# Block transposes for five more heads' worth of probabilities, and a reordered tail, in a post-layer-norm attention and mixture-of-experts kernel

## The chip, the cores and the metric

The kernel runs on one core of a Trainium2 chip. The metric is device time in microseconds (us); three timed runs of the kernel before are listed below. Engines are named as in the profile: PE is TensorE (matmuls and transposes), DVE is VectorE, ACT is ScalarE, POOL is GpSimd, and SP is the engine that issues most DMAs.

## The reference, cut to what matters

All arrays are float32. The input x has shape (2, 1024, 256).

```python
# first layer, then a second layer-norm around the sum
x = layernorm(x + (attention_1_head(layernorm(x)) + x))      # causal, width 256
# second layer
a = attention(layernorm(x))          # 16 heads of 128, causal, rotary on q and k
h = x + a                            # a has the output projection wo and the bias bo
m = moe(layernorm(h))                # softmax gate, best 2 of 4 experts, 256 -> 256 -> 256, exact gelu
out = layernorm(x + (h + m))
```

For each head the second attention computes `scores = q k^T / sqrt(128)`, masks above the diagonal, takes a softmax over each row and multiplies the probabilities with v. Note that x enters the last line twice: once in h, and once as the residual around the layer.

## The kernel before, in words

**Units and steps.** Tokens are cut into 8 tiles of 128 rows per batch. The first layer has 16 rows of tiles (batch 0, then 1), the second has 32 units (a unit is one batch and one head) of 8 rows each. A row of tiles is a step: steps 0 to 15 are the first layer, and step A0 = 16 begins unit 0. Two units that share a batch and a group of weights make a pair; there are 16 pairs. `step(t, fillers)` writes out the instructions of a step in one fixed order, for all engines; each engine works through its own instructions in that order, so an instruction that waits holds up what is behind it on its engine. `at`, `mid`, `first`, `end_of`, `late` and `spread` hang other work onto steps: projections, weight loads, output projections, the first work of the mixture of experts.

**A row of attention.** `RowB.scores` (L703) multiplies q and k into a PSUM tile `sc` (two buffers). `softmax_row` takes the causal minimum (DVE, L329) and the row maximum (DVE, L331); ACT takes the exponential and its sum (L336). `normalise` takes the reciprocal (DVE, L715) and scales the row. Then the row's probabilities must be transposed, since the product with v (`output`, L773, tile `av`) contracts over the keys. There are two ways:

- The PE way (units 0 to 2 and 29 to 31): DVE scales the row (L719); `transposed_row` makes one PE transpose per 128x128 tile (L348), up to four into one PSUM tile, and ACT (L353) or DVE (L351) copies it to `pT`. The product with v follows three steps after the scores (lag 3).
- The block way (`self.blocks`, units 3 to 28, from `U0, U1 = 3, 29`): ACT scales the row (L717); DVE transposes 32x32 blocks (L728) into a staging buffer, `pair_sb` for rows 0 to 3 and the buffer of x1 for rows 4 to 7; and `gather` issues, on SP's queue, 16 DMAs for every four rows (L752) that bring the blocks to their places in `pT`. The product with v has lags of 8 to 10 steps (`PARTS`; lag 7 for unit 28).

Rows 0 to 3 and rows 4 to 7 of a unit are called its first and second half (j = 0 and 1). Row i has i + 1 tiles.

**Buffers with two uses.** The buffer x1 holds the first layer's result. `x1_out` stores it to DRAM (POOL's queue, step 42) before units 3 and later use the buffer for their blocks; `x1_back` loads it again in unit 29 (step A0 + 29*8 + 4). `pair_sb` also holds normalised tiles (`xn_tile`) before unit 3 and from unit 30 on.

**Around it.** `a_residual` finishes the first layer's normalisation in place in x1 (POOL, L438) and adds bo to make h (POOL, L441); for batch 1 this stands at steps 33 to 40. `seven_products` projects q, k and v with seven block products in place of eight; when `wide`, one of its accumulators is taken from the pool `ps_tr` and the order is another. `rotated` applies the rotary embedding to a finished half of q or k: two DMAs on SP's queue swap halves into `rot`, and one step later three POOL operations combine them (L479, L480, L481). `b_output` adds a pair's output projection to h.

**The tail.** From unit 30 on, batch 0's mixture of experts begins among the attention: `m_norm` normalises h (and has POOL add x1 to each tile of h, L1065), `m_transposed` and `gate_products` prepare it, and `hidden` (L1172, L1180) and `expert` (L1196, L1205) run experts 0 and 1 of the first half-batch at steps s + 2 to s + 6 of unit 31. What follows the last row is a list of calls written out by hand: `m_bias`, `m_stats`, `all_of` (one expert on four tiles: 16 matmul records and four DVE additions), and, last, batch 1.

Of the kernel before, what the change touches and what calls it, by code (L numbers as in the profile page):

```python
# [18 lines left out]
P = 128  # L19
# [7 lines left out]
def kernel(  # L27
# [377 lines left out]
    xn1, rr = {}, {}  # L405
# [15 lines left out]
    def a_rfinish(b, j):  # L421
        r = rr[b, j]
        nc.vector.reciprocal(r, r)
        xn1[b, j] = xn_tile()
# [9 lines left out]
    def a_residual(b, i):  # L434
# [3 lines left out]
        nc.gpsimd.tensor_scalar(  # L438
            t, t, mv_a[b][:, i, 0:1], rr[b, i // 4][:, 0, k : k + 1], ALU.subtract, ALU.mult
# [30 lines left out]
    def rotated(t, cs):  # L470
# [6 lines left out]
        def rest():  # L477

            nc.gpsimd.tensor_tensor(t[:, cs], t[:, cs], rope_sb[:, 0, cs], ALU.mult)  # L479
# [4 lines left out]

    BUFS = {"wq": 3, "wk": 4}
# [57 lines left out]
    def seven_products(g, b, name, wide):  # L543
# [46 lines left out]
        def done(i, k):  # L590
            if not value:
                rotated(head_tile(heads[i - 1], name), ts(k - 1, 512))
# [63 lines left out]
    def b_output(g, b, tiles):  # L656
# [17 lines left out]
    U0, U1, GP = 3, 29, 2  # L674
    R1, XB = 33, 4
    PARTS = (
        {8: range(0, 4)},
        {8: range(0, 2), 9: range(2, 4), 10: range(4, 8)},
    )
    LAGS = (11, 10, 9, 8, 7, 3)  # L680

    class RowB:


        def __init__(self, u, i):
            self.u, self.i = u, i
            k = units.index(u)
            self.blocks = U0 <= k < U1

            self.parts = {}  # L690
            if i % 4 == 3:
                self.parts = {3: range(i + 1)}
                if self.blocks:
                    self.parts = {7: range(i + 1)} if k == U1 - 1 else PARTS[i // 4]

# [190 lines left out]
    for i in range(NT):  # L886
        late(9 + i, a_residual, 0, i)
        late(R1 + i, a_residual, 1, i)
# [28 lines left out]
    for k, (g, b) in enumerate(pairs):  # L917
# [3 lines left out]
        wide = U0 <= k * GH < U1  # L921
# [19 lines left out]
        if k:  # L941
# [3 lines left out]
            else:  # L945
                spread(s0, own + outputs, (2, 2, 2, 2, 2, 2, 2, 1))
                at(s1, load_weights, g, ("wo",))
# [75 lines left out]
    def x1_out():  # L1023
        nc.gpsimd.dma_start(x1_dram, x1)

    def x1_back(b):
        nc.gpsimd.dma_start(x1[:, ts(b, NT), :], x1_dram[:, ts(b, NT), :])

    at(R1 + NT + 1, x1_out)
    for b in range(B):  # L1030
        at(A0 + U1 * NT + XB, x1_back, b)
    at(A0 + 28 * NT, load_second, range(3))
    at(A0 + 30 * NT + 4, load_second, (3,))
# [24 lines left out]
    def m_norm(b, j):  # L1058

        xn = xn_tile()  # L1060
        for k in range(4):
# [3 lines left out]
            nc.gpsimd.tensor_tensor(ht, ht, x1[:, b * NT + i, :], ALU.add)  # L1065
        xn2[b, j] = xn

# [183 lines left out]
    at(s + 4, hidden, 0, 0, 1)  # L1251
    at(s + 5, expert, 0, 0, [(0, k) for k in range(4)])
# [126 lines left out]
```

## Time and profile before

| | us |
|---|---|
| median of three runs | 1210.44 (1210.01, 1210.44, 1216.87) |
| the profiled execution's own time | 1212.35 |
| span of the profiled execution | 1210.6 |
| PE busy | 1173.9 |
| DVE busy | 786.9 |
| ACT busy | 633.7 |
| POOL busy | 614.7 |
| PE transposes of probabilities, both layers (L348, 288) | 43.9 |

The span runs from the first to the last instruction; 1.75 us of the profiled time lie outside it. Busy time of PE counts each matmul from its start to its modelled end, and consecutive matmuls overlap, so a long row of matmuls shows as one stretch. A float32 matmul is recorded as two instructions, a transpose as one. Where a unit begins is read from the first of its eight instructions on L329: unit 1 at about 159 us, unit 2 at 197, unit 3 at 231, unit 4 at 259, unit 5 at 284, unit 28 at 937, unit 29 at 969, unit 30 at 1007, unit 31 at 1047, and the last row of unit 31 at 1083.

### The profile page before, as it was taken

The page shows a single profiled execution, that of the slowest core. Times are in us where ns is not written, and L with a number is a line of the kernel's source. Part 1 is how long each engine was busy: PE and PEld are TensorE (multiplying, and loading weights), DVE is VectorE, ACT ScalarE, POOL GpSimd, SP SyncE. Part 2 cuts the span into 40 slices and gives each one's busy share as a digit, 9 for nine tenths or more (in the row PEclk, how much of TensorE's full clock was granted, in tenths as well). Part 3 has the DMA queues.
Part 4 walks back from the last instruction along what each step waited for, and adds up shares of the span by engine and source line. Part 5 has one row for each costly group of instructions (what it writes and reads, how often), then busy time and mean ns, then how long its engine had stood idle before and what let it go on. Part 6 is the DMA issues. An engine that isn't in the chain of part 4 may idle for free.

```text
span 1210.6 us, 15641 instructions
## 1 busy us (share of the span) xinstructions
PE 1173.9 (97%) x4570; PEld 744.1 (61%) x4570; DVE 786.9 (65%) x1810; ACT 633.7 (52%) x1181; POOL 614.7 (51%) x600
## 2 busy tenths in 40 slices
PE   7999989999999999999999999999999999999997
PEld 5676646565656566665656565656566557666665
DVE  5555657676666676666666666676676556677576
ACT  3344434566565565656565656665565544443423
POOL 4036379966564747384746556575848482101000
PEclk9999989999999999999999999999999999999999
DMA  5001112267766767667666676676767870000001
GB/s 180 1 1 36 31 31 61 53 200 161 167 159 156 164 152 166 146 158 161 157 155 162 160 161 157 165 168 159 171 154 173 171 201 32 34 1 1 18 17 35
DMA packets 210949, 140.18 MB, mean 116 GB/s; under 512 B 18764, under 2 KB 192912, under 8 KB 210480
## 3 DMA queue, kind: packets, MB, share of 16 engines
q1 hardware_dynamic: 207616, 129.05, 45.8%
q0 software_dynamic: 2160, 9.08, 2.1%
q10 hardware_dynamic: 1088, 1.05, 0.3%
q8 instruction: 37, 0.61, 0.2%
q14 instruction: 48, 0.39, 0.1%
HBM read 19.57 MB, written 4.19 MB: 20 GB/s over the span
## 4 chain that ended last, share of the span: by engine, by line
PE 88%; DVE 6%; DMA 2%; ACT 1%; SPq 1%; issue 1%; POOL 1%; DVEq 0%; POOLq 0%; ACTq 0%
PE av L773 21%; PE sc L703 19%; PE pa L563 11%; PE pa L660 7%; PE pa L554 5%; PE pc L563 4%; PE pa L1172 4%; PE pa L392 3%; PE sc L370 3%; PE pa L1196 2%; PE pt L348 2%; PE pc L554 2%; PE pe L1196 2%; DVE nmx L331 1%; PE pa L311 1%; PE pa L298 1%
## 5 line engine op out<-in xcount | busy, mean ns | idle before, releaser
L336 ACT ACTIVATE pr<-sc,nmx 128x128 f32<-128x128 f32 (+7 forms) x272 | 200.9, 739 | 190.9 <-DVE nmx L331 128.7
L703 PE MATMUL sc<-Twk,Twq 128*128 128x512 f32 (+3 forms) x768 | 290.6, 487 | 0.0
L773 PE MATMUL av<-pT,vg 128*128 128x512 f32 (+3 forms) x768 | 268.3, 489 | 6.9 <-DMA wq_g<-in_L_ffn_wq_dram 2.9
L717 ACT ACTIVATE pr<-pr,rs 128x128 f32<-128x128 f32 (+1 forms) x208 | 161.3, 775 | 149.9 <-DVE rs L715 149.8
L773 PEld LDWEIGHTS av<-pT,vg 128*128 128x128 f32 x768 | 143.1, 191 | 127.9 <-issue 98.8
L331 DVE TENSOR_REDUCE nmx<-sc 128x1 f32<-128x128 f32 (+7 forms) x272 | 206.1, 758 | 9.4
L703 PEld LDWEIGHTS sc<-Twk,Twq 128*128 128x128 f32 x768 | 138.9, 191 | 114.1 <-issue 101.2
L479 POOL TENSOR_TENSOR Twk<-Twk,rope_sb 128x512 f32<-128x512 f32 x64 | 81.6, 1275 | 222.6 <-DMA rot<-Twk 196.2
L329 DVE TENSOR_TENSOR sc<-sc,limit 128x128 f32<-128x128 f32 x272 | 79.9, 294 | 149.4 <-PE sc L703 136.0
L480 POOL TENSOR_TENSOR rot<-rot,rope_sb 128x512 f32<-128x512 f32 x128 | 165.1, 1290 | 0.0
L728 DVE STREAM_TRANSPOSE x<-pr 128x640 f32<-128x640 f32 (+1 forms) x104 | 108.0, 1039 | 39.1 <-DMA rot<-Twq 17.9
L660 PE MATMUL pa<-wo_g,aT 128*128 128x256 f32 x512 | 126.0, 380 | 0.6 <-ACT aT L789 0.3
L660 PEld LDWEIGHTS pa<-wo_g,aT 128*128 128x128 f32 x512 | 95.5, 190 | 33.7 <-issue 17.2
L479 POOL TENSOR_TENSOR Twq<-Twq,rope_sb 128x512 f32<-128x512 f32 x64 | 81.7, 1277 | 40.9 <-DMA rot<-Twq 30.4
L481 POOL TENSOR_TENSOR Twq<-Twq,rot 128x512 f32<-128x512 f32 x64 | 81.8, 1278 | 5.0
L481 POOL TENSOR_TENSOR Twk<-Twk,rot 128x512 f32<-128x512 f32 x64 | 81.2, 1269 | 5.0
L789 ACT ACTIVATE aT<-av,par 128x512 f32<-128x512 f32 x64 | 43.9, 686 | 64.4 <-PE av L773 64.4
L670 DVE TENSOR_TENSOR hx<-hx,pa 128x256 f32<-128x256 f32 (+1 forms) x124 | 52.2, 425 | 30.7 <-PE pa L660 28.9
L1065 POOL TENSOR_TENSOR hx<-hx,x 128x256 f32<-128x256 f32 x16 | 12.2, 791 | 103.6 <-DVE pair_sb L208 103.6
L588 ACT ACTIVATE part<-pa,par 128x512 f32<-128x512 f32 x64 | 43.8, 686 | 36.9 <-PE pa L563 36.8
L1172 PE MATMUL pa<-xT,we_sb 128*128 128x512 f32 x128 | 58.4, 596 | 2.0 <-DVE hx L1205 1.9
L728 DVE STREAM_TRANSPOSE pair_sb<-pr 128x128 f32<-128x128 f32 (+1 forms) x104 | 52.2, 502 | 3.5 <-DMA wq_g<-in_L_ffn_wq_dram 3.0
(194 smaller groups left out, 1690.4 us busy)
## 6 DMA issues: line engine op xcount, KB each, us to landing
pT<-x SPq DMA_DIRECT2D x416, 128.0 KB, 2.5
pT<-pair_sb SPq DMA_DIRECT2D x416, 64.0 KB, 2.0
rot<-Twk SPq DMA_DIRECT2D x128, 128.0 KB, 2.3
rot<-Twq SPq DMA_DIRECT2D x128, 128.0 KB, 2.3
wk_g<-in_L_ffn_wk_dram SPq DMA_DIRECT2D x9, 256.0 KB, 3.1
wq_g<-in_L_ffn_wq_dram SPq DMA_DIRECT2D x9, 256.0 KB, 3.5
wv_g<-in_L_ffn_wv_dram SPq DMA_DIRECT2D x9, 256.0 KB, 2.9
wo_g<-in_L_ffn_wo_dram SPq DMA_DIRECT2D x9, 256.0 KB, 2.9
```

Source lines behind the costliest of these rows:

```text
L331: nc.vector.tensor_reduce(nmx, sc[:, :L], AX.X, ALU.max, negate=True)
L336: nc.scalar.activation(pr[:, :L], sc[:, :L], AF.Exp, bias=nmx, accum_out=sm)
L479: nc.gpsimd.tensor_tensor(t[:, cs], t[:, cs], rope_sb[:, 0, cs], ALU.mult)
L480: nc.gpsimd.tensor_tensor(rot, rot, rope_sb[:, 1, cs], ALU.mult)
L481: nc.gpsimd.tensor_tensor(t[:, cs], t[:, cs], rot, ALU.add)
L563: nc.tensor.matmul(pa, lhsT=w, rhs=x, start=start, stop=True, skip_group_check=True)
L660: nc.tensor.matmul(pa[:, ts(k, D)], lhsT=aT[g, b][:, hh, ts(i, P)], rhs=wg["wo"][:, hh, :], start=(hh == 0), stop=(hh == GH - 1),)
L703: nc.tensor.matmul(sc[:, ds(n0, n)], lhsT=qT[:, ts(i, P)], rhs=kT[:, ds(n0, n)], start=True, stop=True,)
L717: nc.scalar.activation(self.pr[:, :L], self.pr[:, :L], AF.Copy, scale=rs)
L728: nc.vector.transpose(z[:, i % 4, :n, :], self.pr[:, : n * 32].rearrange("p (m s) -> p m s", s=32))
L773: nc.tensor.matmul(cut(av), lhsT=vg[g, b][:, c, ts(hh, HD)], rhs=cut(pT[:, c, :]), start=(c == 0), stop=(c == i),)
L1172: nc.tensor.matmul(ph, lhsT=we1_sb[:, e, c, ts(m, P)], rhs=x2T[:, c, ds(k0 * P, 512)], start=(c == 0), stop=(c == DC - 1),)
```

## The change

Unit 1, 2 and 29 take the block way for both halves, units 30 and 31 for their second half. That moves `x1_out` to steps 20 and 25, on ACT's queue, one batch each, and `x1_back` behind the last gather, on SP's queue. `a_residual` does its normalisation on ACT (with a small product `nb` on DVE for the bias), and batch 1's stands at steps 17 to 24. For the keys of pair 1 the first of the three rotary operations goes from POOL to DVE. Pair 1 becomes `wide`. In the last pair the value products are spread one to a row and the output projections move into unit 31; `hidden` of expert 0 moves into unit 30, that of expert 1 by one step, and the two experts' second products and four tiles of the output projection move behind the last row. The product with v for the second half of unit 31 is called by hand, behind expert 2's. POOL's addition of x1 moves out of `m_norm` into `m_residual`, called after `x1_back`.

```diff
 def a_rfinish(b, j):
         nc.vector.reciprocal(r, r)
+        nb = small.tile([P, 4], F32, tag=f"nb{b}{j}", name="nb", bufs=1)
+        nc.vector.scalar_tensor_tensor(
+            nb, mv_a[b][:, 4 * j : 4 * j + 4, 0], -1.0, r[:, 0, :], ALU.mult, ALU.mult
+        )
+        nbs[b, j] = nb
 def a_residual(b, i):
-        nc.gpsimd.tensor_scalar(
-            t, t, mv_a[b][:, i, 0:1], rr[b, i // 4][:, 0, k : k + 1], ALU.subtract, ALU.mult
+        nc.scalar.activation(
+            t, t, AF.Identity, bias=nbs[b, i // 4][:, k : k + 1], scale=rr[b, i // 4][:, 0, k : k + 1]
         )
         nc.gpsimd.tensor_tensor(h[:, b * NT + i, :], t, bo_sb, ALU.add)
-    def rotated(t, cs):
+    def rotated(t, cs, eng=nc.gpsimd):
-            nc.gpsimd.tensor_tensor(t[:, cs], t[:, cs], rope_sb[:, 0, cs], ALU.mult)
+            eng.tensor_tensor(t[:, cs], t[:, cs], rope_sb[:, 0, cs], ALU.mult)
+    HELP = ("wk",)
         def done(i, k):
-                rotated(head_tile(heads[i - 1], name), ts(k - 1, 512))
+                eng = nc.vector if (g, b) == pairs[1] and name in HELP else nc.gpsimd
+                rotated(head_tile(heads[i - 1], name), ts(k - 1, 512), eng)
-    U0, U1, GP = 3, 29, 2
-    R1, XB = 33, 4
-    PARTS = (
-        {8: range(0, 4)},
-        {8: range(0, 2), 9: range(2, 4), 10: range(4, 8)},
-    )
-    LAGS = (11, 10, 9, 8, 7, 3)
+    NU = B * H
+    U0, U1, GP = 1, (NU - 2, NU), 2
+    END = 99
+    PARTS = {
+        0: {8: range(0, 4)},
+        1: {8: range(0, 2), 9: range(2, 4), 10: range(4, 8)},
+        (NU - 3, 0): {7: range(0, 4)},
+        (NU - 3, 1): {9: range(0, 8)},
+        (NU - 2, 1): {7: range(0, 8)},
+        (NU - 1, 0): {4: range(0, 4)},
+        (NU - 1, 1): {END: range(0, 8)},
+    }
+    LAGS = (10, 9, 8, 7, 4, 3)
-            self.blocks = U0 <= k < U1
+            self.blocks = U0 <= k < U1[j]
...
-        late(R1 + i, a_residual, 1, i)
+        late(17 + i, a_residual, 1, i)
-        wide = U0 <= k * GH < U1
+        wide = 0 < k < len(pairs) - 1
-                spread(s0, own + outputs, (2, 2, 2, 2, 2, 2, 2, 1))
-                at(s1, load_weights, g, ("wo",))
+                spread(s0, own, (1, 1, 1, 2, 2, 0, 0, 0))
+                spread(s1, outputs, (0, 2, 2, 2, 2, 0, 0, 0))
+                at(s1 + 5, load_weights, g, ("wo",))
-    def x1_out():
-        nc.gpsimd.dma_start(x1_dram, x1)
+    def x1_out(b):
+        nc.scalar.dma_start(x1_dram[:, ts(b, NT), :], x1[:, ts(b, NT), :])
     def x1_back(b):
-        nc.gpsimd.dma_start(x1[:, ts(b, NT), :], x1_dram[:, ts(b, NT), :])
+        nc.sync.dma_start(x1[:, ts(b, NT), :], x1_dram[:, ts(b, NT), :])
-    at(R1 + NT + 1, x1_out)
-    for b in range(B):
-        at(A0 + U1 * NT + XB, x1_back, b)
+    at(A0 + 4, x1_out, 0)
+    at(A0 + 9, x1_out, 1)
-    at(A0 + 30 * NT + 4, load_second, (3,))
+    at(A0 + 30 * NT + 6, load_second, (3,))
 def m_norm(b, j):
-            nc.gpsimd.tensor_tensor(ht, ht, x1[:, b * NT + i, :], ALU.add)
+    def m_residual(b, tiles):
+        for k in tiles:
+            ht = h[:, b * NT + k, :]
+            nc.gpsimd.tensor_tensor(ht, ht, x1[:, b * NT + k, :], ALU.add)
+    mid(s - 2, hidden, 0, 0, 0)
-    at(s + 2, hidden, 0, 0, 0)
-    at(s + 4, hidden, 0, 0, 1)
-    at(s + 5, expert, 0, 0, [(0, k) for k in range(4)])
-    at(s + 6, expert, 0, 0, [(1, k) for k in range(4)])
-    at(s + 7, b_output, G - 1, 1, (0, 1))
-    at(s + 7, b_output, G - 1, 1, (2, 3))
+    at(s + 5, hidden, 0, 0, 1)
-    step(end, [lambda: hidden(0, 0, 2)])
+    step(end, [])
+    for i in (0, 2):
+        b_output(G - 1, 1, (i, i + 1))
     m_bias(0, (3, 4))
+    step(end + 1, [lambda: all_of(0, 0, 0)])
+    step(end + 2, [lambda: hidden(0, 0, 2)])
+    m_bias(0, (5,))
+    for b in range(B):
+        x1_back(b)
     m_stats(1, J0)
-    step(end + 1, [lambda: hidden(0, 0, 3)])
-    m_bias(0, (5,))
-    step(end + 2, [lambda: all_of(0, 0, 2)])
+    all_of(0, 0, 1)
+    hidden(0, 0, 3)
+    all_of(0, 0, 2)
+    steps[end - 1][0].output(END)
+    hidden(0, 1, 0)
     for i in (4, 6):
         b_output(G - 1, 1, (i, i + 1))
+    m_residual(0, ALL)
     m_stats(1, J1)
     m_sqrt(1, ALL)
-    hidden(0, 1, 0)
     m_rstd(1, ALL)
     m_norm(1, 0)
     m_norm(1, 1)
+    m_residual(1, ALL)
     all_of(0, 0, 3)
```

More of the change, by code (lines that the diff above doesn't have):

```diff
@@ L403, in output @@
                 a_finish(b, i // 4)
-    xn1, rr = {}, {}
+    xn1, rr, nbs = {}, {}, {}
     def a_finish(b, j):
@@ L686, in __init__ @@
             self.u, self.i = u, i
-            k = units.index(u)
-            self.blocks = U0 <= k < U1
+            k, j = units.index(u), i // 4
+            self.blocks = U0 <= k < U1[j]
             self.parts = {}
             if i % 4 == 3:
-                self.parts = {3: range(i + 1)}
-                if self.blocks:
-                    self.parts = {7: range(i + 1)} if k == U1 - 1 else PARTS[i // 4]
+                self.parts = PARTS.get((k, j)) or (PARTS[j] if self.blocks else {3: range(i + 1)})
         def scores(self):
```

## The prediction, made before the changed kernel was run

> **What bounds the kernel.** I read the page's busy shares, then busy time by stage (cut where units begin), then the waits of PE, then single instructions in order of time.
>
> ```profile
> PE 1173.9 (97%) x4570; PEld 744.1 (61%) x4570; DVE 786.9 (65%) x1810; ACT 633.7 (52%) x1181; POOL 614.7 (51%) x600
> ```
>
> PE is nearly always busy, but busy ends are modelled, so the stages decide. Columns: length, then busy time and count of PE, weight loads, DVE, ACT, POOL; granted clock; DMA.
>
> ```profile
> 159.00:197.00 38.00, 34.63 (x122) 19.45 (x120) 23.00 (x43) 15.77 (x34) 29.04 (x25) 0.91 0.24 56
> 197.00:231.00 34.00, 32.27 (x144) 20.17 (x144) 23.99 (x47) 15.29 (x33) 32.43 (x32) 1.00 0.17 40
> 231.00:259.00 28.00, 27.68 (x105) 17.34 (x105) 19.36 (x44) 15.27 (x32) 26.25 (x27) 1.00 0.56 178
> 259.00:284.00 25.00, 23.17 (x97) 13.97 (x96) 17.86 (x39) 16.32 (x31) 9.20 (x8) 1.00 0.65 148
> 284.00:314.00 30.00, 30.00 (x106) 18.58 (x105) 19.45 (x46) 17.32 (x33) 23.75 (x22) 1.00 0.73 167
> 314.00:341.00 27.00, 27.00 (x113) 16.79 (x112) 18.41 (x41) 17.58 (x34) 11.31 (x12) 1.00 0.70 157
> ...
> 1007.00:1047.00 40.00, 36.83 (x199) 27.25 (x197) 30.28 (x78) 17.77 (x36) 7.53 (x10) 1.00 0.08 27
> ```
>
> The rows at 284 and 314 are one settled pair of block units: PE has no idle time, DVE and ACT have 9 to 13 us to spare per unit. There a microsecond of PE work removed is a microsecond of time. The first rows are units 1 to 4, where the PE way ends and the block way begins: PE idles 7.25 of 125 us. The last row is unit 30, on the PE way.
>
> **The transposes that go.** A unit has 1+2+...+8 = 36 transposes, its second half 5+6+7+8 = 26; so 3x36 + 2x26 = 160 go.
>
> ```profile
> L348 PE MATMUL pt<-ident,pr 128*128 128x128 f32 x288 | 43.9, 279 | 3.6 <-DVE xT L217 1.5 <-DVE pT L351 1.0 <-ACT xT L219 0.8
> ```
> ```profile
> 1095.02 1.04 PE L348 MATMUL pt<-ident,pr 128*128 128x128 f32 x8
> ```
>
> The group gives 43.9/288 = 0.152 us each, which counts each burst's last latency. In order of time, eight take 1.04 and one alone 0.27, so each further one costs 0.77/7 = 0.11. PE runs on into other work, so I take 0.11: 160 x 0.11 = **-17.6** (bounds -17.6 and -24.4): 72 of them, -7.9, at the start, 88, -9.7, at the end.
>
> What takes their place: per full unit 16 block transposes in two shapes, whose means of 0.50 and 1.04 make 4x0.50 + 4x1.04 = 6.2 us on DVE, in place of 5.6 of scaling (L719, 0.70 x 8) and 1.9 of copies; ACT gains 8 x 0.775 = 6.2 and loses 8 x 0.50 of copies; SP gains 32 DMAs at about 0.65, 21 us in a unit of 28. The settled units carry exactly this with PE never idle, so I cost it at nothing there; it counts where PE has little other work, at both ends of the attention.
>
> The Trainium skill ("VectorE: DVE Perf Modes", Rules for kernel authors) speaks against the change: it gives a 128x128 transpose to TensorE when PSUM will do as the target, since DVE only turns 32x32 blocks, and its section on the three transpose paths warns of strided DMA copies. This trace has both ways: a row's block transpose takes 1.24 us against 1.04 for eight on PE, so by the rule the change gains nothing; but DVE has the room and PE has not, so I keep the row's answer.
>
> **Start (units 1 to 4).** Apart from the transposes only order changes: with lags of 8 to 10 the products with v leave unit 1 for later units, 2.6 us of them. The waits of PE there:
>
> ```profile
> PE pa L563 <- DVE Twk L595: 2.4, 1, 2.4
> PE pc L554 <- ACT part L586: 1.5, 1, 1.5
> PE pt L348 <- DVE xT L217: 1.5, 1, 1.5
> PE pa L563 <- DVE rs L715: 1.2, 1, 1.2
> PE pt L348 <- DVE pT L351: 1.0, 2, 0.7
> ```
>
> The 2.4 at 161 us is DVE's: two subtractions of x blocks (0.90, 1.75), unit 0's last scaling (1.56) and an addition. All stay, so it stays, and so does the slow clock behind it. The 1.0 waits on a copy of the PE way and goes; of the other 4.2 a light unit will have its like (unit 4, the first with little product work, has the 1.5 now). I take -2.5 in all for waits (bounds: +3, one more wait like the 2.4; -7, all idle time).
>
> POOL is busy 61.5 of 72 us in units 1 and 2. It loses 16 scalings in the first layer's residual (1.27 each), 8 of them at 207 to 245 us, and four rotary products (1.27 each, 5.1 us in unit 1); batch 1's eight additions (0.74, 5.9 us) come earlier, mostly into its gaps of 14 and 4.7 us. ACT's 16 residuals of 128x256 are bounded by its scaling of that size, 0.51, and its copy, 0.37: 6 to 8 us, in stages where ACT is busy 22 of 56 and 17 of 40 us; without that cover half a microsecond per step. The four products `nb` are 128x4, like L416 (0.67, twice 0.16): 1 to 3 us of DVE, hidden by PE. DVE's four rotary products have L540's shape: 0.68 to 1.75, so 3 to 7 us in unit 1. With them I count 26 us of DVE in unit 1 against 25 of PE, so unit 1 is even and its waits stay. `x1_out` took 8.8 us for both batches; the second, issued near 167, lands by 176, and the first block transpose into x1 is five steps later, near 181. Two issues on ACT's queue are 1 us. Start: -7.9 - 2.5 = **-10.4**.
>
> **End (unit 29 on).** Gains: -9.7, and waits of unit 30 that go because value products come one per row (1.1 on vg) and POOL no longer adds beside DVE's normalising (0.8; L208 takes 0.41 alone, 0.82 beside POOL): -2. `x1_back` leaves unit 29, where nothing waited for it.
>
> Losses: two places. **The last gather.** Counted from the end of the last scores on PE, DVE has: maximum 1.5, bias additions 4x0.52, block transposes of rows 5 and 6 (0.97, 1.11, with 1.0 of waiting for ACT's scaling), two output additions 1.3, bias additions 8x0.52, four expert additions 1.7, row 7's transpose 1.24: together 15. SP then issues 16 gathers at 0.65, 10.4, and the last lands 2.5 later:
>
> ```profile
> pT<-x SPq DMA_DIRECT2D x416, 128.0 KB, 2.5
> ```
>
> So the product may start at 28. PE has until then: first-half product 2.6 and six pieces of 3.45 (output projection, three expert products, two hidden layers): 23.3. PE waits about **+5** in all, in one piece or several (bounds: 0 if PE itself comes late, at 28; 10, the whole issue time). **The normalising chain.** Now, from the last output projection (PE ends at 1109.0) to the fourth normalised tile (1114.8) is 5.8 us, and two pieces on PE, 6.9, cover it. `hidden` of the next half moves ahead of the projection, so 3.45 cover 5.8: **+2.4**, and +0.6 for a PSUM bank freed later (0 to 4). `x1_back` (7.2 us) and POOL's first four additions (0.8 each) end near 28+10.4 = 39, before DVE's expert additions near 50; if they did not, DVE would wait, and PE with it. Sum of the end: -9.7 - 2 + 5 + 3 = **-3.7**.
>
> A wait of this size can cost more than itself:
>
> ```profile
> 161.60:164.10 2.50, 0.11 (x1) 0.00 (x0) 2.46 (x5) 0.00 (x0) 2.42 (x3) 0.79 0.00 0
> 164.10:167.00 2.90, 2.88 (x7) 1.74 (x8) 1.42 (x5) 1.69 (x4) 1.07 (x3) 0.50 0.41 90
> 167.00:170.00 3.00, 3.00 (x9) 1.88 (x8) 1.43 (x3) 0.62 (x2) 2.80 (x3) 0.52 0.00 0
> ```
>
> After 2.4 us without work the granted clock was half for 5.9 us: 2.9 us more. The waits of 1.7 and 1.5 had no such tail. I leave it out of the middle value and keep +3 in the range. The Trainium skill ("TensorE: Matmul & The Clock Gate", Part 1) puts the gate at an idle window of about 3.4 us; by it neither new wait would add anything, by the row one of them may add 2.9.
>
> **Sum.** -10.4 - 3.7 = -14.1. On the profiled execution's own 1212.35 that is 1198.2; this execution was 1.9 above the median of 1210.44, to which the same difference gives **1196**.
>
> **Rivals.** (a) *Nearly all of it comes through*: transposes at 0.11 to 0.152 and the start's waits gone, tail covered: -18 to -25, 1186 to 1192. For it: settled units hide all of this. Against: the tail has less cover. (b) *The tail eats its part*: gather 10 and chain 4, plus half clock 3, against -11.7: the end is +5, and the start alone remains: -5, 1205. (c) *Slower*: DVE's rotary products in unit 1 stand in order behind nothing but the `rot` transfers, in place of POOL, which idled 196.2 us in 34 waits for them, 5.8 each. If DVE waits 5.8 four times, PE (two score buffers) stops with it: 4x5.8, plus 2.9 of half clock each, is +35 against -14: 1231. It decides once a transfer lands later than DVE's arrival one step on by over 2 us. Against it: the transfer takes 2.3 and a step over 3; POOL merely came early. (d) *PE's time is not the limit at either end* (DVE and the queues are): the transposes leave as idle time, 0 to -4, 1208.
>
> **How the numbers follow.** Forecast (1190 to 1201) 0.54, (a) 0.15, (b) 0.18, (c) 0.07, (d) 0.06. The range leaves out (c), (d) and the outer part of (a): 1186 to 1207. About 1%, 12 us, is what a measurement of this kernel can tell: faster means under 1198.3. That takes two thirds to four fifths of the forecast and all of (a): 0.60; slower is (c), 0.07; the rest is 0.33.
>
> **What would show it.** L348 falls from 288 to 128 and unit 1's second half is in L728; units 1 to 4 take about 115 us together; the half clock of unit 1 is still there; PE waits ahead of the last product with v, with DMA named, and ahead of batch 1's transposes with L208 named. I am wrong if PE's waits in unit 1 name `rot`, if unit 29 is not near the 30 us of the settled unit at 284, or if the tail has more than 9 us of new waits.

## The result, and the profile after

| | us, median (lowest to highest) | runs |
|---|---|---|
| before, on the same chip | 1213.37 (1209.2 to 1218.47) | 12 |
| after | 1214.18 (1212.0 to 1217.75) | 12 |

The ratio is 1.0003, 95% interval 0.9985 to 1.0021: the change moves the time by nothing that can be measured, where 1196 was forecast. The profiled execution of after took 1212.0, with a span of 1210.2; of before 1212.35 and 1210.6.

The two profiles are not equally typical. The mean granted clock of after's 12 runs lies between 0.988 and 0.995 (median 0.991), and the profiled run, the fastest of them, has 0.995. Before's profile has 0.995 too, but the 30 runs of it that stand beside the first experiments have a median of 0.997. An estimate from these numbers: 0.006 of 1212, some 7 us of clock, is lost in a typical run of after and not in one of before, and the two profiles side by side do not show it.

The busy line of the page after:

```profile
PE 1158.6 (96%) x4410; PEld 727.3 (60%) x4410; DVE 782.1 (65%) x1798; ACT 652.0 (54%) x1197; POOL 587.1 (49%) x577
```

PE's busy time fell by 15.3 us and its instructions by 160, and the span stayed. The group of transposes (here with its releasers, from the groups of PE) has lost 160 of 288, as forecast, and gained a wait for the scaled row:

```profile
L348 PE MATMUL pt<-ident,pr 128*128 128x128 f32 x128 | 19.9, 276 | 7.3 <-DVE pr L732 5.4 <-DVE xT L217 1.5 <-ACT aT L802 0.3
```

The chain that ended last, by engine, before and after: a share of 14% of the span, 170 us, has gone over from PE to queues, transfers and the other engines. These shares say which way the chain runs, not what it costs: in the fastest kernel of the next section PE's share is 63%.

```profile
PE 88%; DVE 6%; DMA 2%; ACT 1%; SPq 1%; issue 1%; POOL 1%; DVEq 0%; POOLq 0%; ACTq 0%
```
```profile
PE 74%; SPq 8%; DVE 7%; DMA 5%; POOL 4%; issue 2%; ACT 1%; POOLq 0%; DVEq 0%; ACTq 0%
```

Busy time by stage after, cut where units 0, 1, 2, 3, 4, 5 and 6 begin and in the tail (columns as in the prediction):

```profile
119.00:165.00 46.00, 38.34 (x164) 25.42 (x162) 33.48 (x64) 22.04 (x43) 26.05 (x29) 1.00 0.16 46
165.00:195.00 30.00, 27.47 (x91) 14.32 (x92) 22.09 (x46) 16.04 (x32) 21.98 (x20) 1.00 0.36 99
195.00:226.00 31.00, 25.20 (x97) 14.87 (x97) 20.97 (x44) 17.10 (x33) 19.40 (x20) 0.94 0.66 153
226.00:261.00 35.00, 31.30 (x105) 18.73 (x104) 19.06 (x42) 17.05 (x33) 26.62 (x25) 0.95 0.81 175
261.00:288.00 27.00, 27.00 (x112) 16.63 (x111) 18.42 (x41) 17.29 (x34) 6.75 (x6) 1.00 0.57 131
288.00:318.00 30.00, 29.70 (x103) 18.11 (x102) 19.22 (x43) 16.85 (x32) 22.97 (x22) 1.00 0.72 166
...
1068.00:1210.00 142.00, 127.37 (x472) 85.63 (x470) 90.17 (x240) 45.91 (x60) 11.41 (x16) 0.98 0.15 45
```

PE now idles 7.7 us in unit 0 and 5.8 in unit 2, and in units 2 and 3 the granted clock fell to 0.94 and 0.95; unit 4 runs like a settled one. Busy ends are modelled, so for the comparison I count PE's own work in another way: each matmul at the median distance from its start to the next start for its shape, in that trace. What is left of a stage is waiting or slow clock. The count runs from PE's first to its last instruction, about 1199 us in both traces; what is left in the first and last cell of a column leaves out the time before and after. Each cell is length / what is left, in us, from one profile (start only, tail only and best kernel are kernels of the next section; the best one is its last).

| stage | before | after | start only | tail only | best kernel |
|---|---|---|---|---|---|
| up to unit 0 | 118.7 / 6.1 | 120.3 / 6.6 | 119.3 | 118.8 | 119.2 / 5.6 |
| unit 0 | 40.0 / 3.0 | 45.1 / 9.1 | 45.1 / 9.2 | 40.0 | 39.8 / 3.8 |
| unit 1 | 38.5 / 7.2 | 29.7 / 3.1 | 29.9 | 38.7 | 30.8 / 4.8 |
| unit 2 | 34.0 / 2.4 | 31.1 / 8.4 | 32.3 / 9.7 | 34.1 | 28.7 / 5.3 |
| unit 3 | 27.8 / 0.4 | 35.1 / 5.6 | 34.8 / 5.6 | 28.8 | 31.0 / 1.6 |
| unit 4 | 25.4 / 2.4 | 26.7 / 0.0 | 27.0 | 24.9 | 26.8 / 0.0 |
| units 5 to 27 | 652.9 / 6.0 | 652.5 / 4.8 | 653.8 | 654.5 | 655.8 / 8.9 |
| unit 28 | 31.5 / 4.8 | 28.0 / 1.0 | 28.6 / 1.8 | 32.8 / 6.1 | 27.9 / 1.3 |
| unit 29 | 38.2 / 0.8 | 30.9 / 1.6 | 40.5 | 29.5 | 30.6 / 1.1 |
| unit 30 | 39.7 / 4.7 | 36.5 / 5.8 | 39.6 | 37.4 / 6.8 | 35.3 / 4.7 |
| unit 31 | 36.4 / 1.6 | 32.3 / 1.7 | 36.4 | 32.3 | 32.3 / 1.7 |
| after the last scores | 127.5 / 4.5 | 142.2 / 12.8 | 127.3 | 141.9 / 12.3 | 136.6 / 7.2 |

In all, PE's own work fell from 1155.1 to 1138.7, by 16.4, and the rest rose from 43.9 to 60.3, by 16.4. The gain is there and is given back whole, mainly at four places: unit 0 (+6.1), unit 2 (+6.0), unit 3 (+5.2) and the tail (+8.3); units 1, 4 and 28 lost 10.3 us of waiting on the other side. The longest waits of PE in units 0 to 5 after:

```profile
PE pt L348 <- DVE pr L732: 5.4, 3, 2.5
PE av L786 <- DMA pT<-pair_sb: 4.1, 1, 4.1
PE av L786 <- DMA pT<-x: 3.7, 1, 3.7
PE pc L561 <- ACT part L593: 1.7, 1, 1.7
```

and from unit 29's end on:

```profile
PE pa L1190 <- DVE hx L1223: 4.8, 3, 2.0
PE av L786 <- DMA pT<-pair_sb: 3.3, 1, 3.3
PE av L786 <- DMA pT<-x: 2.9, 2, 1.6
PE pt L214 <- DVE pair_sb L208: 1.3, 3, 0.5
```

At three of the four places the name at the head is new: the scaled row and, twice, a gather. PE waited for the experts' sums in before's tail too, but less:

```profile
PE pa L1172 <- DVE hx L1205: 1.9, 2, 1.5
```

Behind some of the waits the granted clock was half for 3.4 us, a loss of 1.7 us each time. After has three such stretches, behind the waits of 4.1, 3.7 and, in the tail, 2.0; behind the wait of 2.5 in unit 0, which ends at 165.3, there is none:

```profile
165.30:168.70 3.40, 2.23 (x11) 1.35 (x11) 3.33 (x8) 2.12 (x5) 3.24 (x6) 1.00 0.09 39
208.00:211.40 3.40, 3.40 (x7) 1.86 (x6) 2.19 (x6) 1.29 (x3) 3.32 (x4) 0.50 0.94 224
255.80:259.20 3.40, 3.40 (x6) 1.44 (x5) 2.38 (x5) 2.14 (x3) 3.32 (x5) 0.50 0.59 135
1119.30:1122.70 3.40, 3.40 (x11) 2.05 (x9) 0.00 (x0) 1.28 (x2) 0.00 (x0) 0.51 0.00 0
```

Before has 6.8 us of half clock from 163.0 and 3.4 from 951.5, of which PE was waiting for 1.1. So the two profiles happen to lose nearly the same by it: about 4.6 us before, 5.1 after. The experiments ask who makes each wait long.

### The profile page after: what moved, and what is told of

The parts are those of the page before. It is cut to its first block, busy times and chain, and to the rows that moved or that the text cites. A ratio compares the mean times of both kernels' runs of the same rounds, so it can differ in the third digit from the quotient of the medians.

```text
span 1210.2 us, 15511 instructions
## 1 busy us (share of the span) xinstructions
PE 1158.6 (96%) x4410; PEld 727.3 (60%) x4410; DVE 782.1 (65%) x1798; ACT 652.0 (54%) x1197; POOL 587.1 (49%) x577
## 4 chain that ended last, share of the span: by engine, by line
PE 74%; SPq 8%; DVE 7%; DMA 5%; POOL 4%; issue 2%; ACT 1%; POOLq 0%; DVEq 0%; ACTq 0%
PE av L786 18%; PE sc L716 14%; PE pa L570 8%; SPq L765 7%; PE pa L668 6%; PE pa L561 5%; PE pa L1190 4%; PE pc L570 3%; DMA pT<-x 3%; PE sc L370 3%; PE pa L392 2%; PE pc L561 2%; PE pe L1214 1%; PE pa L1214 1%; DVE pair_sb L208 1%
## 5 line engine op out<-in xcount | busy, mean ns | idle before, releaser
L786 PE MATMUL av<-pT,vg 128*128 128x512 f32 (+3 forms) x768 | 272.1, 493 | 18.7 <-DMA pT<-x 8.8
L730 ACT ACTIVATE pr<-pr,rs 128x640 f32<-128x640 f32 (+1 forms) x240 | 187.7, 782 | 179.4 <-DVE rs L728 179.2
L485 POOL TENSOR_TENSOR Twk<-Twk,rope_sb 128x512 f32<-128x512 f32 x60 | 76.4, 1273 | 199.2 <-DMA rot<-Twk 175.7
L741 DVE STREAM_TRANSPOSE x<-pr 128x640 f32<-128x640 f32 (+1 forms) x124 | 128.8, 1039 | 54.4 <-DMA pT<-x 32.0
L485 POOL TENSOR_TENSOR Twq<-Twq,rope_sb 128x512 f32<-128x512 f32 x64 | 81.5, 1273 | 46.0 <-DMA rot<-Twq 27.3
L802 ACT ACTIVATE aT<-av,par 128x512 f32<-128x512 f32 x64 | 43.9, 686 | 46.1 <-PE av L786 46.1
L595 ACT ACTIVATE part<-pa,par 128x512 f32<-128x512 f32 x62 | 42.6, 687 | 39.5 <-PE pa L570 39.4
L741 DVE STREAM_TRANSPOSE pair_sb<-pr 128x128 f32<-128x128 f32 (+1 forms) x116 | 58.2, 502 | 3.6 <-issue 3.4
L447 POOL TENSOR_TENSOR hx<-x,bo_sb 128x256 f32<-128x256 f32 x16 | 12.2, 763 | 99.5 <-ACT x L444 99.5
```

The lines of the kernel that those rows point to most:

```text
L485: eng.tensor_tensor(t[:, cs], t[:, cs], rope_sb[:, 0, cs], ALU.mult)
L730: nc.scalar.activation(self.pr[:, :L], self.pr[:, :L], AF.Copy, scale=rs)
L741: nc.vector.transpose(z[:, i % 4, :n, :], self.pr[:, : n * 32].rearrange("p (m s) -> p m s", s=32))
L786: nc.tensor.matmul(cut(av), lhsT=vg[g, b][:, c, ts(hh, HD)], rhs=cut(pT[:, c, :]), start=(c == 0), stop=(c == i),)
```

## The experiments

**The two halves apart.** First the start alone, made from before: block way from unit 1, residual on ScalarE and 16 steps earlier, rotary products for pair 1's keys on VectorE, `x1_out` early (the diff shows only the steps). Then the tail alone, made from after with all of that undone.

```diff
-    U0, U1, GP = 3, 29, 2
-    R1, XB = 33, 4
+    U0, U1, GP = 1, 29, 2
+    R1, XB = 17, 4
```
```diff
-    U0, U1, GP = 1, (NU - 2, NU), 2
+    U0, U1, GP = 3, (NU - 2, NU), 2
-    HELP = ("wk",)
+    HELP = ()
-        late(17 + i, a_residual, 1, i)
+        late(33 + i, a_residual, 1, i)
```

> The kernel before with the start of the change alone: blocks from unit 1 on, the first layer's residual on ScalarE and at steps 17 to 24, the two early stores of x1, DVE's part of the key rotation, pair 1 wide; the tail as before. Theory S (the start's removed transposes, 72 x 0.11 = 7.9 us, come back as new waits in units 0, 2 and 3): units 0 to 4 take 167 to 169 us as in the changed kernel (before 165.8), the whole within 4 us of before. Rival R (the start gives the 10 us of the prediction, and it is lost by what the start does to the tail): 8 to 11 us faster than before.

Measured: 1219.24 (1215.33 to 1223.54, 8 runs) against 1211.6 (30 runs) of before, ratio 1.006 (1.0039 to 1.0082). The start alone costs 0.6%, so rival R falls. Theory S has units 0 to 4 right (169.1 us), but not the whole: 7.6 us slower, where S allowed 4. Its profile shows 3.4 of them in units 0 to 4 and 2.3 in unit 29; the profiled run is 2.6 us faster than the median, and the rest was not looked for. Its column shows the waits of units 0, 2 and 3 in full, and unit 28's wait gone: so that gain comes with the start and not with the tail.

> The changed kernel with the start of before (blocks from unit 3 on, residual on GpSimd at steps 33 to 40, one store of x1 at step 42) and the changed tail. Theory S: units 29 to the end as in the changed kernel, 242 us against 241.7 before, so the whole within 3 us of before; the 3.5 us that unit 28 gained in the changed profile, if they come with the tail, make it up to 4 us faster. Rival R: 10 us slower than before.

Measured: 1210.87 (12 runs), ratio 0.9993 (0.9979 to 1.0008). The tail alone is worth nothing either: units 29 to 31 are 15 us shorter (99.2 for 114.3) and what follows them 14.4 longer, of which 7.8 is waiting. The two halves fail independently. Their costs do not add up, though: +7.6 and -0.7 stand against about +1 for both together, and why is open.

**Unit 2: the gather of unit 1's first half.** PE comes to the product with v at 203.5; the last transfer lands at 207.3. The issues on SyncE's queue after, in order of time (the second column is the time that all of a row's issues took):

```profile
190.74 6.26 SPq L765 DMA_DIRECT2D pT<-pair_sb  x8
197.12 0.53 SPq L480 DMA_DIRECT2D rot<-Twq  x1
197.69 0.59 SPq L481 DMA_DIRECT2D rot<-Twq  x1
198.40 0.52 SPq L467 DMA_DIRECT2D wk_g<-in_L_ffn_wk_dram  x1
199.06 0.46 SPq L480 DMA_DIRECT2D rot<-Twq  x1
199.56 0.60 SPq L481 DMA_DIRECT2D rot<-Twq  x1
200.20 5.59 SPq L765 DMA_DIRECT2D pT<-pair_sb  x8
```

The gather's second eight stand behind the query's transfers and a weight load. So they were issued at once, right behind the first eight:

```diff
+                if row.u == units[1] and row.i == 3:
+                    if k == 0:
+                        row.gather(0)
+                        row.gather(1)
```

> The changed kernel, with both halves of the gather of unit 1's first four rows issued in one step, ahead of the two key or query swaps and the weight load that stand between them now. Theory Q (SP's queue in order: the second eight gathers stood behind transfers that waited for products of the next step): the wait of 4.1 us at unit 2's first product with v falls under 1.5, the half clock behind it goes, units 0 to 4 lose 4 to 6 us. Rival P (PE is early there, with little product work in units 1 and 2, and the gather begins only after DVE's fourth transpose): the wait stays above 3 us, nothing gained.

Measured: 1219.19 (9 runs), ratio 1.0051 (1.0035 to 1.0068). The wait for the gather fell to 0.3, as theory Q has it, but units 0 to 4 took 171.4 us (167.7 in after): a longer wait stands in its place.

```profile
PE sc L716 <- POOL Twq L487: 6.7, 2, 6.0
```

Now the query's transfers stand behind 16 gathers, the rotation comes late, and the scores wait 6.0 us. The queue takes one issue after another, and unit 2, with 22.7 us of its own work, reaches both needs before the queue has served either. My reading is that whichever goes second loses.

**Unit 3: the experts' load.** Unit 3's wait is for `pT<-x`, unit 2's second half, whose first eight gathers are issued from 236.5 on. At 235.3 GpSimd issues `load_experts`, 1 MB, which the change left at step A0 + 24, where no gather was before. It was moved to step A0 + 5:

```diff
-    at(A0 + 3 * NT, load_experts)
+    at(A0 + 5, load_experts)
```

> The changed kernel with the load of the experts' first weights (1 MB) 19 steps earlier, at step A0+5, where no gather runs. Theory C (in unit 3 that load slows the gathers: they land 8 us after their issue instead of 2.5): the wait of 3.7 us in unit 3 goes with its half clock, 4 to 6 us less. Rival I (the 16 issues at 0.65 us and the swaps on SP's queue are too slow for the lag by themselves): the wait stays above 2.5 us, at most 1 us less.

Measured: 1210.28 (10 runs), ratio 0.9982 (0.9961 to 1.0003), which does not tell it from before. Unit 3 falls from 35.1 to 29.5 with nothing left over. The transfers of that stretch, from issue to landing, after:

```profile
pT<-x SPq DMA_DIRECT2D x9, 128.0 KB, 7.2
we_sb<-in_L_ffn_we_dram POOLq DMA_DIRECT2D x1, 1024.0 KB, 9.3
```

and with the load moved away:

```profile
pT<-x SPq DMA_DIRECT2D x8, 128.0 KB, 2.6
```

The load on another queue made a gather take 7.2 us instead of 2.6, and SyncE's next issues late as well (the second eight begin at 246.45, without the load at 243.93): shown, since this load is the only thing that was moved. The second eight, all issued after the load had landed at 244.5, still took 4.4 us (2.4 without it).

**Unit 0: GpSimd's order.** GpSimd's addition of bo (L447) follows ScalarE's new residual (L444) in batch 1, and stands ahead of its rotary products. After, GpSimd and VectorE:

```profile
139.53 0.73 POOL L447 TENSOR_TENSOR hx<-x,bo_sb 128x256 f32<-128x256 f32 x1 [12.02 <-ACT x L444]
140.22 1.26 POOL L485 TENSOR_TENSOR Twk<-Twk,rope_sb 128x512 f32<-128x512 f32 x1
141.44 1.27 POOL L486 TENSOR_TENSOR rot<-rot,rope_sb 128x512 f32<-128x512 f32 x1
142.79 1.26 POOL L487 TENSOR_TENSOR Twk<-Twk,rot 128x512 f32<-128x512 f32 x1
```
```profile
140.49 1.02 DVE L426 SCALAR_TENSOR_TENSOR nb<-mva,rx 128x4 f32<-128x4 f32 x1
141.43 2.78 DVE L208 TENSOR_SCALAR pair_sb<-x,mva,rx 128x256 f32<-128x256 f32 x2
```

Before, GpSimd's three rotary products ran from 136.65 to 140.5 and VectorE's two normalising pieces after them, at 140.96, took 0.73 together. After, they run side by side and the pieces take 2.78 (1.44 and 1.42), each ending 0.15 us behind a GpSimd instruction of 1.27; the row's scaling stands behind them. So the additions were put two steps later:

```diff
-        nc.gpsimd.tensor_tensor(h[:, b * NT + i, :], t, bo_sb, ALU.add)
+        if b == 0:
+            a_bias(b, i)
+        late(19 + i, a_bias, 1, i)
```

> The changed kernel, with GpSimd's 8 additions h = x1 + bo of batch 1 put two steps later than ScalarE's residual, so that GpSimd's queue does not stand waiting for ScalarE (in the changed kernel it waits until 139.53 us and its rotary products then run at 140 to 150 us, beside VectorE's normalising pieces, L208, of 1.36 to 1.44 us each; before they were 0.41). Theory T1 (GpSimd's queue, held by ScalarE, slides onto VectorE): the pieces come back near 0.41 us, the waits of unit 0 for the normalised row (5.4 us in 3) mostly go, unit 0 falls from 45.1 to 40 or 41 us; the wait of unit 1 for the rotated k may come back (up to 2.4). Rival (the added work on ScalarE and VectorE itself is what costs): unit 0 stays at 45 us, within 1.

Measured: one run of 1207.24 beside one of 1208.64 of before; the stage decides. Unit 0 is 39.5 us (45.1), GpSimd's first product starts at 136.16, and VectorE's pieces:

```profile
140.47 0.23 DVE L426 SCALAR_TENSOR_TENSOR nb<-mva,rx 128x4 f32<-128x4 f32 x1
140.63 0.73 DVE L208 TENSOR_SCALAR pair_sb<-x,mva,rx 128x256 f32<-128x256 f32 x2
```

T1 holds: ScalarE's and VectorE's added work is all still there and costs nothing that unit 0 shows (40.0 in before); the wait that it put into GpSimd's queue cost 5.6 us.

**Unit 2 again: the product a step later.** With the experts' load early as well:

```diff
+        (1, 0): {9: range(0, 4)},
```

> The changed kernel with the experts' load early (as in the run before) and the attention product of unit 1's first half one step later, nine steps after its row instead of eight. Theory Q (SyncE's queue holds the gather, landed 207.3 us, when the light unit 2 wants it at 202.9): one step of unit 2 is about 3.2 us, so the wait falls from 4.1 us to about 1, the half clock after it goes, unit 2 falls from 31.1 to about 27 or 28 us and nothing else moves; units 0 to 4 about 158 us. Rival (the wait only moves on to the next product or to the scores behind the query's transfers, as with the gather in one step): unit 2 stays within 1.5 us of 31.

Measured: 1210.52, one run, before 1208.64. Unit 2 stays at 31.0: the rival is right. The product no longer waits; the scores do, for the rotated query:

```profile
PE sc L717 <- POOL Twq L487: 3.9, 2, 3.2
```

That the transfers for it landed at 202.7 and the rotation began at 204.6 shows who is next: GpSimd's four instructions on the sums of wk (L537 to L540), which had themselves waited for their weights until 202.2, stand ahead of it.

**The tail: the last row first.** After, VectorE ahead of the last block transpose:

```profile
1074.66 1.26 DVE L678 TENSOR_TENSOR hx<-hx,pa 128x512 f32<-128x512 f32 x2
1075.85 4.00 DVE L1177 SCALAR_TENSOR_TENSOR hx<-lent,comb,hx 128x256 f32<-128x256 f32 x8
1079.76 0.87 DVE L1223 SCALAR_TENSOR_TENSOR hx<-pe,comb,hx 128x256 f32<-128x256 f32 x2
1080.54 0.87 DVE L1223 SCALAR_TENSOR_TENSOR hx<-pa,comb,hx 128x256 f32<-128x256 f32 x2
1081.33 1.24 DVE L741 STREAM_TRANSPOSE x<-pr 128x1024 f32<-128x1024 f32 x1
```

The row was scaled by 1076.0 and stood 5.3 us behind the bias and an expert's sums.

```diff
-    m_bias(0, (3, 4))
-    step(end + 1, [lambda: all_of(0, 0, 0)])
+    step(end + 1, [])
+    all_of(0, 0, 0)
     step(end + 2, [lambda: hidden(0, 0, 2)])
-    m_bias(0, (5,))
+    m_bias(0, (3, 4, 5))
```

> The changed kernel with the last row's block transpose on VectorE ahead of two pieces of the experts' bias (8 instructions of 0.48 us) and of the first expert's combination. Theory L (the last row is late because VectorE's order puts 3.8 us of bias and the combination ahead of it): the transpose ends about 77 us instead of 82.6 (counted from 1000), the gather lands about 90 instead of 95.2, the product's wait of 1.6 us and the 1.5 us wait for hx before it go, and the tail is 2 to 3 us shorter (142.2 to about 139.5). Rival (TensorE finds other waits on VectorE there, which has the same work to do before it): tail within 1 us of 142.2.

Measured: 1214.68, one run, before 1208.64; the tail 141.5 (142.2). The transpose ran 5.3 us earlier and both waits went, as L has it; but the bias now stands ahead of the second expert's sums, and PE waits 2.05 for those (5.4 in 3 for hx, where after had 4.8). The rival is right: a wait on VectorE's order was moved, not removed.

**The tail: GpSimd's residual additions.** `m_residual` runs beside the last normalising, as the additions in `m_norm` did in before. The eight pieces took as long there (first line: before; second: after), but PE then waited only 0.4 us on them:

```profile
1112.64 5.14 DVE L208 TENSOR_SCALAR pair_sb<-hx,mvh,rsh 128x256 f32<-128x256 f32 x8
1111.61 5.13 DVE L208 TENSOR_SCALAR pair_sb<-hx,mvh,rsh 128x256 f32<-128x256 f32 x8
```

```diff
-    m_residual(0, ALL)
     m_stats(1, J1)
...
     m_norm(1, 1)
-    m_residual(1, ALL)
     all_of(0, 0, 3)
+    m_residual(0, ALL)
+    m_residual(1, ALL)
```

> The changed kernel with GpSimd's 16 residual additions (0.72 to 0.82 us each) put after the last normalising and the fourth expert's combination, so that none runs beside VectorE's normalising pieces. Theory S (a VectorE piece of 0.41 us takes 0.81 when GpSimd's two-input addition runs beside it): the six slow pieces come back to 0.41, the last ends 2.4 us earlier, the waits for them (0.40 and 0.40) go and the 2.0 us wait for hx shrinks by about 1.5: tail shorter by 1.5 to 2.5 us, unless the sums are then late for the output. Rival (VectorE is slow there for another reason): pieces stay at 0.81, tail within 0.5 us.

Measured: 1210.98, one run, before 1208.64; the tail 138.7 (142.2), more than S expected. The eight pieces:

```profile
1114.19 2.68 DVE L208 TENSOR_SCALAR pair_sb<-hx,mvh,rsh 128x256 f32<-128x256 f32 x8
```

S holds: 5.13 to 2.68 us, and the waits behind them go from 3.3 to 0.9. The half clock behind the wait of 2.0 goes with it, 1.7 us, which S did not count. So this run shows a cure, not what the change made worse: the slow pieces were there before, with more work of PE over them.

**All together.** The cures that held, and for the places where the wait only moved, the next one behind it: the sums of wk three steps later, the first expert's products ahead of the output projection, all of the bias in VectorE's idle time behind the last gather. For unit 30's 3.3 us, the first eight of unit 29's gather went to another queue.

```diff
-                at(before + (1 if k == 1 else 4), weight_sums, "wk")
+                at(before + 4, weight_sums, "wk")
+                    q = nc.scalar if (units.index(self.u), j, part) == (NU - 3, 0, 0) else nc.sync
+    all_of(0, 0, 0)
     for i in (0, 2):
         b_output(G - 1, 1, (i, i + 1))
...
     steps[end - 1][0].output(END)
+    m_bias(0, (3, 4, 5))
```

> The changed kernel with the cures of the runs before together, and three new ones: GpSimd's additions of batch 1 two steps later; the experts' load early; unit 1's first-half product a step later and, new, GpSimd's three block sums of wk for that pair three steps later, behind the rotation that the scores of unit 2 wait for; new, the first eight of unit 29's first-half gather on ScalarE's DMA queue (SyncE's stands full from 982 to 1014 us); GpSimd's residual additions after the last normalising; and, new, the first expert's combination ahead of the output projection, the last row's transpose ahead of all of the bias, and three pieces of the bias (12 instructions, 5.8 us) put into VectorE's idle 12 us after the last gather. Theory W (the transposes' 16.4 us are gone, and what came back are these waits, each with a cause of its own): unit 0 back to 39.5 us (-5.6), unit 2 to 26 or 28 (-3 to -5), unit 3 to 29.5 (-5.6), unit 30 to 33 or 34 (-3), tail 142.2 to about 136 (-6): together -22 to -25, so about 1190 us, and faster than the kernel before by 1.5 to 2%. Rival V (VectorE or GpSimd is at its limit at both ends, and a wait taken away at one place comes back at the next): less than half of it, 1203 us or more.

Measured: 1201.76 (1200.5 to 1205.19, 6 runs), before 1211.34 (11 runs), ratio 0.9933 (0.9912 to 0.9953). Faster by 0.7%, clear of the noise, but 9.6 us and not the 22 to 25 that W had: less than half, as rival V has it, though not V's 1203. By stage W holds for unit 0 (39.8), unit 2 (28.2), unit 30 (33.7) and the tail (136.4); unit 3 took 31.1, and unit 29 got a new wait of 7.7 and took 39.8:

```profile
PE av L792 <- DMA pT<-x: 8.7, 2, 7.7
```

ScalarE there, and SyncE's queue:

```profile
977.65 5.31 ACTq L771 DMA_DIRECT2D pT<-pair_sb  x8
983.10 1.01 ACT L336 ACTIVATE pr<-sc,nmx 128x896 f32<-128x896 f32 x1 [4.92 <-DMA rot<-Twq]
```
```profile
969.62 5.81 SPq L771 DMA_DIRECT2D pT<-x  x8
979.90 0.51 SPq L484 DMA_DIRECT2D rot<-Twq  x1
```

Eight issues held it for 5.3 us, and the exponential, whose input was ready at 979.1, stood behind them. But what PE waits for is a gather on SyncE's queue, and SyncE issued nothing from 975.4 to 979.9. Its next issue waits for the semaphore that ScalarE's first gather signals when it lands, at 979.82 (both issues use the same one; with all issues on SyncE's queue, in the next run, there is no such pause), and the last eight gathers come that much later. Two more kernels: the eight back on SyncE's queue, and on GpSimd's.

```diff
-                    q = nc.scalar if (units.index(self.u), j, part) == (NU - 3, 0, 0) else nc.sync
+                    q = nc.gpsimd if (units.index(self.u), j, part) == (NU - 3, 0, 0) else nc.sync
```

> The kernel of the run before with the eight gather issues of unit 29 back on SyncE's queue; all else as there. Theory H (those eight issues held ScalarE for 0.62 us each, 4.9 us, and the exponential, the query's transfers and the second half's gather behind them came late, so that unit 29 waited 7.7 us): unit 29 falls from 39.8 to about 31, unit 30 goes back from 33.7 to about 37.5, together -5, so about 1197 us and 1.1 to 1.3% faster than the kernel before. Rival (another of the edits, GpSimd's or SyncE's, made unit 29's wait): unit 29 stays above 36, time within 2 us of 1202.

> The same, with those eight issues on GpSimd's queue. Theory H': GpSimd is held by about 0.7 us each, 5 us, in a stretch in which its rotations are not wanted for some 10 us, SyncE's queue is relieved by as much: unit 29 about 31, unit 30 about 34 to 35 with the wait for unit 29's first half (3.3 us) gone, so 3 us below the run with all on SyncE, about 1194. Rival (GpSimd's rotations and block sums come late instead, and scores or values wait for them): units 29 and 30 together no shorter than with all on SyncE.

Measured, before 1210.72 (11 runs): on SyncE's 1199.31 (6 runs), ratio 0.9898 (0.9869 to 0.9926); on GpSimd's 1196.75 (1195.21 to 1197.41, 4 runs), ratio 0.9879 (0.9849 to 0.9909). Without ScalarE's issues unit 29 falls to 34.0, not to 31, so those eight made the larger part of it, 5.8 us, and H's rival falls; that holding ScalarE did it, rather than SyncE's pause, is not shown. A wait of 2.4 with half clock behind it stays, where after had 1.3; its cause is open. On GpSimd's queue units 29 and 30 take 65.9 us, for 70.5 on SyncE's and 73.5 on ScalarE's. That does not show H': 3.4 of the 4.6 us are two stretches of half clock that the one profile has and the other has not, unit 30's wait is 2.1 there and 1.6 with all on SyncE's queue, and the two kernels' times overlap.

So versions with all that the change does, and nothing taken back but orders and queues, are 1.0% and 1.2% faster than before. PE's own work in the last is 1137.5, 17.6 below before, and what is left is 46.1, for 43.9 before. In its profile the clock never falls to half before PE's last instruction, so none of the 46.1 is slow clock, while before's 43.9 hold some 4.6 us of it. The four runs have a mean clock of 0.997 to 0.999, where after's twelve have 0.988 to 0.995: by these numbers, and as an estimate, up to 9 of the 17 us between after and this kernel are clock that the waits had cost besides their own length. Whether the same orders would help the kernel before was not tried; the largest of the waits that they remove are not in its trace, the slow normalising pieces are.

## Why the prediction was wrong

*The transposes (-17.6, at 0.11 each): right.* PE's own work fell by 16.4, by 17.6 in the best kernel; from unit 29 on by 9.8, for 9.7. A unit has 8 block transposes and not the 16 of the prediction's sentence; its sum of 6.2 us counts 8.

*"The settled units carry exactly this with PE never idle, so I cost it at nothing there; it counts where PE has little other work, at both ends": this is the step that failed.* In units 5 to 27 it is right (652.9 to 652.5). For units 1 to 4, where by its own words it should count, the sum held no price for it at all, and took 2.5 of waits off instead. Its transposes are there to a tenth: PE's own work in units 1 to 4 fell by 7.8. But what is left of those units rose from 12.4 to 17.1, +4.7 for -2.5, so that they took 122.6 us and not 115; and unit 0, which the sum left out, took 5.1 more. The -10.4 came as +1.9, which is most of the miss. Three terms:

- Unit 2 has 22.7 us of PE's own work, and SyncE needs about 21 of issues for a unit's gathers besides the query's transfers. The prediction had both kinds of number and did not set one against the other. About 6 us, of which the best kernel has 3.1 back; that the queue makes the rest is argued from these two numbers, not shown.
- Unit 3's experts' load is not in the diff. That the block way now reaches back to where it lands was a resource newly shared, and of what else the transfer engines carry in that stretch the prediction counts `x1_out` alone. About 5 us, gone when the load was moved.
- Unit 0: batch 1's eight additions were counted as moving "mostly into its gaps". They did fit; but each brought a wait for ScalarE to the head of GpSimd's queue, and what stood behind them was not named. About 6 us, all given back by the two-step shift.

*"All stay, so it stays" (the 2.4 of unit 1 and its half clock): wrong.* Unit 1's wait for Twk is 1.5 and its clock 1.00; a wait of 2.5 stands in unit 0 instead, without a half clock behind it.

*The half clock, left out of the middle value:* it is in no sum of the start or the end, and three stretches of it, 5.1 us, stand behind new waits, while before's two, some 4.6 us, went. The sentence that by a window of 3.4 us neither new wait would add anything does not follow from its own numbers, since a wait of 5 in one piece is longer than that; as it came, the waits of the tail were 2.0 or less, and one of 2.0 did add 1.7.

*The last gather (row 7 transposed 15 after the last scores, landed at 28, +5): right.* The scores end at 1067.9, the transpose at 1082.6, the last transfer lands at 1095.2: 14.7 and 27.3. The waits up to there are 1.0 + 1.5 + 1.6 = 4.1.

*The normalising chain (+3): the mechanism right, the closeness of the sum in part luck.* The waits on it are 0.5 + 0.4 + 0.4 for the tiles, forecast at 2.4, and 2.0 for the sums that free a PSUM bank, forecast at 0.6: together 3.3. As forecast, the chain is as long as before (its eight pieces take 5.13 us, 5.14 before) and has 3.45 us of products over it where it had 6.9. That GpSimd's additions double its pieces was so before as well; the run with the additions moved takes all but 0.9 of the waits away by another way.

*Unit 30 (-2): wrong.* What is left of it rose by 1.1: the wait for vg went, and one of 3.3 us for unit 29's first half came. Six other kernels with the same code there took 37.9 to 39.2 us, 1.4 to 2.7 more than after, with half clock behind that wait, which after's profile has not. So the end, forecast at -3.7, came as +0.1. In after's trace SyncE's issues follow one another with no pause above 0.2 us from 979.0 to the last of that gather, at 1005.7; it lands at 1007.7, and PE goes on at 1008.2. The prediction left this queue out at the end too, save for the last gather. That relieving it cures the wait is not shown: it was 2.1 with eight issues on GpSimd's queue and 1.6 with all on SyncE's.

*Of the rivals*, (c) fell: VectorE waited 2.4 us in all for `rot`, in 3 waits. (d), that the transposes leave as idle time, is what happened, at 0.06. It was right in its result; "PE's time is not the limit" says too much, since the same work with other orders gives 1197. That this is near the 1196 forecast is chance: the forecast had none of those orders, and before ran at 1210.72 beside it.

*The rule that speaks against the change* (a 128x128 transpose belongs on TensorE) would have had the right total here, but not for its reason: with other orders the same block transposes leave a gain of 1.2%, so it is queues and orders that took it.

## What to carry to other kernels

When a stage is to take on a working scheme from a settled one, price it in that stage: set each queue's issue time and the time from issue to landing against the stage's own PE time, and list all else, in the diff or not, that uses the same queue or transfer engines in that stretch. When an instruction is moved from one engine to another, ask what its consumer's queue holds behind it. A cure is not done when the wait is gone: look what comes late next, and take that too, before judging. And before a difference between two profiles is read, set the granted clock of each beside that of the kernel's other runs.

## What the runs showed of the hardware that was not expected

- A 128x256 `tensor_scalar` on VectorE takes 0.41 us alone and 1.4 next to a GpSimd two-input instruction of 1.27: it ends just behind it. In the tail, next to ones of 0.77, it takes 0.81, before and after alike. A 128x4 product took 1.02 instead of 0.23. The Trainium skill states this as an exclusive lock on a port pair that the two engines share, held for a whole instruction ("SBUF — State Buffer", Who interferes with whom); the rows agree, and by it unit 0's piece, behind a GpSimd instruction, costs that instruction's rest.
- A 128 KB gather lands 7.2 us (median of nine) after its issue while a 1 MB load on another queue is under way, 2.6 (of eight) without it.
- An issue holds the issuing engine: eight took 5.3 us of ScalarE and 4.4 of GpSimd, whose next instruction began at the end of the last. The skill ("DMA: Bandwidth & Descriptors", Issuing engines are not separate DMA queues) says that issuing from several engines saves only the sequencer's time, usually small; here a unit's 32 issues take about 21 us of SyncE's queue, by the estimate of 0.65 each. And an issue on one queue can wait for a landing on another: SyncE's stood 4.5 us until ScalarE's first gather had landed.
- Half clock came in stretches of 3.4 us or a multiple behind waits of PE, but the length of the wait alone does not decide. The same wait of 2.0 us in unit 0 has a granted clock of 0.50 behind it in the run with the last row first (144.2 to 147.6) and 1.00 in after (145.1 to 148.5). The wait of 3.3 in unit 30 has 0.50 behind it in the run with GpSimd's residual additions later and 1.00 in after. A wait of 3.8 in the run with the additions of bo later has 1.00. So a stage with a wait in it can differ by 1.7 us from one execution to the next.
